# Two orders inside a planned recurrent step: which product comes first in its third tick, and where one relu stands among the evictions

## The chip, the cores and the metric

The kernel runs on one core of a Trainium2 chip. The metric is the device time of one execution in microseconds; lower is better. Engines are named as in the profile: PE is TensorE's matmul, PEld its weight load, DVE is VectorE, ACT is ScalarE, POOL is GpSimd, SP issues DMAs.

## What is computed

The input is 64 graphs of 256 nodes with 256 features (x) and an integer adjacency matrix each (adj). Two residual layers follow each other; the normalisation has no weights. Cut to what matters:

```python
# layer 0: a gated graph network, three steps with shared GRU weights
h = relu(layernorm(x))
for i in range(3):
    m    = h @ weight[i]
    aggr = einsum('bst,bsd->btd', adj != 0, m)
    gi, gh = aggr @ w_ih.T + b_ih, h @ w_hh.T + b_hh
    r = sigmoid(gi_r + gh_r)
    z = sigmoid(gi_z + gh_z)
    n = tanh(gi_n + r * gh_n)
    h = (1 - z) * n + z * h
x = x + h
# layer 1: graph attention, 4 heads of 64
v = (relu(layernorm(x)) @ W.T + b)
logits = leaky_relu(v.a_src[i] + v.a_dst[j], 0.2), masked where adj != 1
x = x + softmax(logits over j) @ v
```

## The kernel before, in words

**Work.** The graphs are taken in 32 pairs. A pair's state is held transposed, `hT`: 128 partitions (features, two chunks) by 512 columns (two graphs of 256 nodes). All products are fp32. Many of the GRU's products are not computed as they stand: the weights are combined beforehand (`w_a`, `w_h`, `w_n`) and sums of states are formed on DVE (`T1`, `T2`, `T3`, `T4`, and `T2n`, `T3n`, `T4n` for the n gate), so that the two graphs of a pair share some products. A call of `block` (L309) is such a product: four matmuls of 128x256, which the trace shows as eight records[...]. A call of `part` (L447) is one matmul (two records) of 128x256.

**The plan.** Every piece of work is a Python function put into `plan` at a tick, which may be a fraction, and a phase: STEP, READY, REST in that order (L322 to L328). At the end the ticks are run through in order (L1033), and the scheduler is manual (L123): what a function emits goes to the end of the queue of its engine. So each engine works in exactly the order in which the functions are called; waits between engines are put in by the framework. A step takes six ticks, `tick_0` to `tick_5` of the class `Step`. A pair has three steps, which start 12 ticks apart, and pairs start 18 ticks apart; so there is always exactly one step in hand, and between its ticks stand the other pairs' normalisation, transposes and attention. The pattern repeats every 18 ticks, that is every three steps. I call those three steps slot A, slot B and slot C, in the order of the trace.

**One step.** `tick_1` makes the part NS2 into one half of the bank `qb` (L482), has DVE write `qb`'s other half from it (L483), makes the block RH into `pc`, the part N01, and has ACT copy `pc` to `pd` (L489); DVE makes T3 and T2. `tick_2` (L494) makes the parts NS3 and NS4 into the two halves of `qb` (L496, L497), has DVE make a piece of `hn` from the first (L498, a scalar_tensor_tensor, "the stt" below) and ACT another from the second (L501, which runs as L451, "state_n"), then the block S1 from T1 into the bank `p5` (L502; the trace writes it `p<-T`), which ACT copies to `m5` (L503, in the trace `m<-p`), and DVE makes T4 (L504). `tick_3` makes the block S2 into `pd`, DVE adds `pd` and `m5` into the bank `pe` (L509, "the pe add"), then the block RA into `pc`. `tick_4` makes the part N11, the block RZ into `pd` (in the trace `pd<-T,w_h`; it overwrites what the pe add reads) and the block S4 into `pe` (it adds to what the pe add wrote). `tick_5` is the n gate and the tail; `update` (L552) makes the new state one step later.

**Beside the step.** When a step has ended, `back` (L788) turns each half of the new state back to nodes with four transposes (bank `pback`, L807), ACT rounds it to `hNhi` (L797) and DVE takes the rest, `hNlo` (L798). It stands in the REST phase of the ticks 1 and 2 of the step that follows; so the second half's `hNhi` and `hNlo` stand right behind `tick_2`. In slot C the last step of a pair has ended, and `residual` (L811) takes their place.

From the third pair on, the first normalisation is made ahead and turned by DMA: `result` makes `xn_a` (L353, four instructions on DVE), a relu in place on ACT follows (L771), and `halve` (L385) splits the result into half words (L387, `words_a`) for a DMA to DRAM and a transposing DMA back. `result` and the relu stand in the READY phase of tick -10 of their pair; that is `tick_2` of another pair's step, in slot B. `halve` stands in the READY phase of tick -9. In slot B stand also ACT's first masks of another pair's logits (L921, 128x1024) at that same tick 2, and the attention values: products `pv` (L863), DVE's `val` (L868) and `score` (L876), and a transpose of the scores on PE, `pscore` (L886).

In slot A stand ACT's leaky relus of the attention (L968) and DVE's row maxima (`any`, L948).

**PSUM.** Five banks rotate for the step (`ps_g`: qa, qb, pc, p5, pd, pe, pn0, pn1), three for all else (`ps_m`).

Of the kernel before, what the change touches and what calls it, by code (L numbers as in the profile page):

```python
# [14 lines left out]
AF = mybir.ActivationFunctionType  # L15
# [3 lines left out]
P = 128  # L19
# [8 lines left out]
def gated_gnn_then_gat_kernel(  # L28
# [39 lines left out]
    nc = tc.nc  # L68
    B, N, D = x.shape
# [4 lines left out]
    KD = D // P  # L74
# [3 lines left out]
    T = PB * N  # L78
# [121 lines left out]
    w_a = [const.tile([P, KD, 6 * D], F32, name=f"w_a_{l}") for l in range(L)]  # L200
    RH, RZ = range(2)
    N00, N01, N11, NS1, NS2, NS3, NS4 = range(7)
    RA, ZA, NA, S1, S2, S4 = range(6)
# [99 lines left out]
    def flat(y):  # L303
        return y.rearrange("q r d -> q (r d)")
# [4 lines left out]
    def block(pt, w, j, src, start=False):  # L309

        for c in range(KD):
            for k in range(KD):
                nc.tensor.matmul(  # L313
                    pt[:, ts(c, N)], w[:, k, j * D + c * P : j * D + (c + 1) * P], src[:, k, :],
                    start=start and c == 0 and k == 0, stop=(c == KD - 1 and k == KD - 1),
                    skip_group_check=True,
                )
# [9 lines left out]
    def at(tick, phase, p, fn):  # L327
        plan.setdefault(tick, ([], [], []))[phase].append((-p, fn))  # L328

    def plan_norm(src, name, p, ticks, relu=False):  # L330


        v = {}

        def stats(r0):
            def fn():
                if not v:
                    v["st"] = small.tile([P, R, 6], F32, tag="st", name=f"st_{name}")
                    v["mv"] = small.tile([P, R, 2], F32, tag="mv", name=f"mv_{name}")
                for r in (r0, r0 + 1):  # L340
                    nc.vector.bn_stats(v["st"][:, r, :], src()[:, r, :])
                    nc.vector.bn_aggr(v["mv"][:, r, :], v["st"][:, r, :])
            return fn

        def deviation():
            rstd = v["rstd"] = small.tile([P, R], F32, tag="rstd", name=f"rstd_{name}")
            nc.vector.tensor_scalar_add(rstd, v["mv"][:, :, 1], EPS)
            nc.gpsimd.tensor_tensor(rstd, rstd, mhalf, ALU.pow)

        def result():  # L350
            xn = v["xn"] = buf("xn", [P, R, D], f"xn_{name}")
            for r in range(R):
                nc.vector.tensor_scalar(  # L353
                    xn[:, r, :], src()[:, r, :], v["mv"][:, r, 0:1], 0.0 if relu else v["rstd"][:, r : r + 1],
                    op0=ALU.subtract, op1=ALU.max if relu else ALU.mult,
                )

        for t, fn in zip(ticks, (stats(0), stats(2), deviation, result)):
            at(t, READY, p, fn)
        return v  # L360

    def plan_relu_T(v, tag, name, p, ticks):

        w = {}

        def fn(k):
            def go():
                if not w:
                    w["hT"] = buf(tag, [P, KD, T], f"hT_{name}")
                pt = bank(f"pt_{name}_{k}")  # L370
                for r in range(R):
                    nc.tensor.transpose(pt[:, ts(r, P)], v["xn"][:, r, ts(k, P)], ident)
                nc.scalar.activation(w["hT"][:, k, :], pt, AF.Relu)
            return go

        for k, t in enumerate(ticks):
            at(t, REST, p, fn(k))
        return w

    def plan_turn(src, tag, name, p, ticks):  # L380


        w = {}

        def halve():  # L385
            words = buf("words", [P, R, 2, D], f"words_{name}", U16)
            nc.vector.tensor_copy(words, src().bitcast(U16).rearrange("q r (d w) -> q r w d", w=2))  # L387
            w["rows"] = dram.tile([R, P, 2 * D], U16, tag="words", name=f"words_dram_{name}")
            nc.sync.dma_start(w["rows"].rearrange("r q e -> q r e"), words.rearrange("q r w d -> q r (w d)"))

        def turn():
            w["turned"] = buf("turned", [P, 2, KD * T], f"turned_{name}", U16)
            nc.sync.dma_start_transpose(
                w["turned"].rearrange("q w (k n) -> q (w k) n", k=KD), w["rows"].rearrange("r q e -> (r q) e")
            )

        def join():
            w["hT"] = buf(tag, [P, KD, T], f"hT_{name}")
            nc.vector.tensor_copy(
                flat(w["hT"]).bitcast(U16).rearrange("q (n w) -> q n w", w=2), w["turned"].rearrange("q w n -> q n w")  # L400
            )

        at(ticks[0], READY, p, halve)
        at(ticks[1], REST, p, turn)
        at(ticks[2], READY, p, join)
        return w
# [4 lines left out]
    def of(y, i):  # L411
        return y[:, :, ts(i, N)]

    class Step:
# [77 lines left out]
            nc.vector.tensor_add(self.own("T2", [P, KD, N]), T3, h0)  # L492

        def tick_2(self):  # L494
            q_b = self.qb
            self.part(q_b[:, :N], NS3, self.T3n)  # L496
            self.part(q_b[:, N:], NS4, of(self.hT(), 1)[:, 1, :])  # L497
            nc.vector.scalar_tensor_tensor(  # L498
                of(self.hn, 1)[:, 1, :], q_b[:, :N], bhn[:, 1:2], self.m5n, op0=ALU.add, op1=ALU.add
            )  # L500
            self.state_n(0, 1, q_b[:, N:])  # L501
            block(self.p5, w_a[self.l], S1, self.T1, start=True)  # L502
            nc.scalar.copy(self.own("m5", [P, T]), self.p5)  # L503
            nc.vector.tensor_sub(self.own("T4", [P, KD, N]), self.T2, of(self.aggr, 0))  # L504

        def tick_3(self):
            R_ = self.own("R", [P, KD, T])
# [232 lines left out]
    def plan_pair(p):  # L740
# [5 lines left out]
        def ready(t, fn):  # L746
            at(t0 + t, READY, p, fn)
# [20 lines left out]
        xn_a = plan_norm(lambda: v["x"], f"a{p}", p, [t0 + t for t in norm_ticks])  # L768
        ready(-1 if p else -2.5, to_edge)
        if dma_a:  # L770
            ready(-10, lambda: nc.scalar.activation(flat(xn_a["xn"]), flat(xn_a["xn"]), AF.Relu))  # L771
            h = plan_turn(lambda: xn_a["xn"], "hT_a", f"a{p}", p, [t0 - 9, t0 - 8, t0 - 3])
        else:
            h = plan_relu_T(xn_a, "hT_a", f"a{p}", p, [t0 - 4, t0 - 3])
# [238 lines left out]
    for p in range(NPAIR):  # L1013
        plan_pair(p)
# [52 lines left out]
```

## Time and profile before

| what | value |
|---|---|
| median of 3 runs | 2521.81 us (2521.77 to 2523.39) |
| the profiled execution | 2522.01 us, span 2520.2 us |
| PE / PEld busy | 2468.9 us (98%) / 2189.5 us (87%) |
| DVE / ACT / POOL busy | 1947.3 us (77%) / 1433.9 us (57%) / 630.3 us (25%) |
| granted TensorE clock | 0.997 |
| a block (eight records), start to start | 1.73 us |
| a part (two records), start to start | 0.43 us |
| a period of three slots | 76.4 us |
| the profile's chain by engine | PE 68%, DVE 23%, ACT 6% |

The period is the distance of two neighbouring `pscore` matmuls in the timeline, 1254.19 and 1330.64 us. A line of a timeline reads: start in the span, duration, engine, line of the kernel, operation, the tile written, the tiles read, shapes, how many instructions are merged, and in brackets the idle time before it and what ended that. In a list of waits, a line reads: who waited for whom, the time in all, how often, the longest.

### The profile page before, as it was taken

The page shows a single profiled execution, that of the slowest core. Times are in us where ns is not written, and L with a number is a line of the kernel's source. Part 1 is how long each engine was busy: PE and PEld are TensorE (multiplying, and loading weights), DVE is VectorE, ACT ScalarE, POOL GpSimd, SP SyncE. Part 2 cuts the span into 40 slices and gives each one's busy share as a digit, 9 for nine tenths or more (in the row PEclk, how much of TensorE's full clock was granted, in tenths as well). Part 3 has the DMA queues.
Part 4 walks back from the last instruction along what each step waited for, and adds up shares of the span by engine and source line. Part 5 has one row for each costly group of instructions (what it writes and reads, how often), then busy time and mean ns, then how long its engine had stood idle before and what let it go on. Part 6 is the DMA issues. An engine that isn't in the chain of part 4 may idle for free.

```text
span 2520.2 us, 37693 instructions
## 1 busy us (share of the span) xinstructions
PE 2468.9 (98%) x13446; PEld 2189.5 (87%) x13446; DVE 1947.3 (77%) x4576; ACT 1433.9 (57%) x3007; POOL 630.3 (25%) x514
## 2 busy tenths in 40 slices
PE   8999999999999999999999999999999999999998
PEld 6888888888888888888888888888888888888887
DVE  5678877788777788777878777887777887778767
ACT  3445556555555555556555555555565555665664
POOL 0112232222222232222232322222222222222222
PEclk9999999999999999999999999999999999999999
DMA  3025656555656455656556565556565556564455
GB/s 95 17 59 126 152 117 143 128 124 127 155 114 150 119 124 137 135 125 145 116 128 149 122 139 131 121 126 159 109 151 120 126 133 135 126 148 118 107 115 109
DMA packets 322091, 313.73 MB, mean 124 GB/s; under 512 B 166560, under 2 KB 282224, under 8 KB 321904
## 3 DMA queue, kind: packets, MB, share of 16 engines
q1 hardware_dynamic: 286608, 181.29, 27.1%
q0 software_dynamic: 33728, 130.03, 26.9%
q8 instruction: 106, 1.74, 0.3%
q14 instruction: 81, 0.66, 0.1%
q10 hardware_dynamic: 1568, 0.01, 0.0%
HBM read 215.62 MB, written 56.60 MB: 108 GB/s over the span
## 4 chain that ended last, share of the span: by engine, by line
PE 68%; DVE 23%; ACT 6%; issue 2%; DMA 1%; POOL 0%; DVEq 0%; SPq 0%; ACTq 0%; POOLq 0%
PE pd L313 16%; PE pn L313 9%; PE pc L313 9%; PE po L572 7%; PE pe L313 6%; PE qb L448 5%; PE pa L470 5%; PE p L313 4%; PE qa L448 3%; DVE any L948 3%; DVE hT_a L558 2%; DVE val L868 2%; DVE edge L763 2%; DVE hNlo L798 2%; PE pback L807 2%
## 5 line engine op out<-in xcount | busy, mean ns | idle before, releaser
L540 POOL TENSOR_TENSOR R<-hT_a,hn 128x512 f32<-128x512 f32 x191 | 278.2, 1457 | 1250.2 <-ACT hn L536 1175.5
L313 PE MATMUL pn<-aggr,w_a 128*128 128x256 f32 x1536 | 365.1, 380 | 1.8 <-DVE pn L525 1.8
L313 PE MATMUL pd<-T,w_a 128*128 128x256 f32 x1536 | 366.3, 381 | 0.0
L313 PEld LDWEIGHTS pn<-aggr,w_a 128*128 128x128 f32 x1536 | 286.9, 190 | 43.2 <-DVE pn L525 3.2
L313 PEld LDWEIGHTS pd<-T,w_a 128*128 128x128 f32 x1536 | 288.1, 191 | 37.6
L557 DVE SCALAR_TENSOR_TENSOR R<-Z,R 128x512 f32<-128x512 f32 x192 | 134.3, 700 | 215.9 <-POOL R L540 207.5
L572 PEld LDWEIGHTS po<-val,zz 128*128 128x128 f32 x2048 | 244.9, 192 | 4.5
L948 DVE CUSTOM_DVE_ANT_0 any<-drow,noedge 128x256 f32<-128x256 f32 x496 | 238.0, 480 | 9.7 <-DMA drow<-score_dram 1.0
L536 ACT ACTIVATE hn<-pn,bi 128x256 f32<-128x256 f32 x384 | 160.3, 470 | 146.0 <-PE pn L313 145.8
L572 PE MATMUL po<-val,zz 128*128 128x65 f32 x2048 | 242.1, 272 | 0.0
L588 POOL TENSOR_TENSOR x<-x,o 128x256 f32<-128x256 f32 x124 | 136.9, 1105 | 393.3 <-DVE o L583 372.1
L968 ACT ACTIVATE zz<-zz,val 128x256 f32<-128x256 f32 x496 | 224.2, 506 | 0.0
L455 ACT ACTIVATE R<-pc,brz 128x256 f32<-128x256 f32 x192 | 80.5, 470 | 241.6 <-PE pc L313 241.6
L798 DVE TENSOR_TENSOR hNlo<-pback,hNhi 128x512 fp32r<-128x512 f32 x128 | 88.2, 689 | 150.4 <-ACT hNhi L797 150.4
L455 ACT ACTIVATE R<-pe,brz 128x256 f32<-128x256 f32 x192 | 80.5, 470 | 216.2 <-PE pe L313 216.2
L525 DVE SCALAR_TENSOR_TENSOR pn<-R,hn 128x512 f32<-128x512 f32 x192 | 148.6, 774 | 49.3 <-ACT R L455 32.0
L313 PE MATMUL pd<-T,w_h 128*128 128x256 f32 x768 | 183.6, 382 | 0.2 <-DVE pe L509 0.2
L313 PE MATMUL p<-T,w_a 128*128 128x256 f32 x768 | 181.4, 379 | 0.0
L313 PE MATMUL pc<-hT_a,w_h 128*128 128x256 f32 x768 | 181.4, 379 | 0.0
L313 PE MATMUL pc<-aggr,w_a 128*128 128x256 f32 x768 | 181.4, 379 | 0.0
L313 PE MATMUL pe<-aggr,w_a 128*128 128x256 f32 x768 | 181.4, 379 | 0.0
L313 PEld LDWEIGHTS pd<-T,w_h 128*128 128x128 f32 x768 | 143.5, 190 | 24.7 <-DVE pe L509 6.4
(183 smaller groups left out, 5254.8 us busy)
## 6 DMA issues: line engine op xcount, KB each, us to landing
zz<-score_dram POOLq DMA_DIRECT2D x62, 1024.0 KB, 11.8
zz<-topT_dram POOLq DMA_DIRECT2D x62, 1024.0 KB, 8.8
adj<-in_adj_dram SPq DMA_DIRECT2D x64, 512.0 KB
drow<-score_dram SPq DMA_DIRECT2D x62, 512.0 KB
x<-in_x_dram SPq DMA_DIRECT2D x32, 512.0 KB
out_dram<-x SPq DMA_DIRECT2D x31, 512.0 KB
words_dram_a<-words_a SPq DMA_DIRECT2D x30, 512.0 KB
words_dram_b<-words_b SPq DMA_DIRECT2D x29, 512.0 KB
```

What stands on the lines that cost most here:

```text
L313: nc.tensor.matmul(pt[:, ts(c, N)], w[:, k, j * D + c * P : j * D + (c + 1) * P], src[:, k, :], start=start and c == 0 and k == 0, stop=(c ...
L448: nc.tensor.matmul(pt, w_n[:, j, :], src, start=start, stop=True, skip_group_check=True)
L455: nc.scalar.activation(of(dst, i)[:, c, :], src[:, c, :], AF.Tanh, bias=brz[:, g0 + c : g0 + c + 1], scale=0.5)
L525: nc.vector.scalar_tensor_tensor(by_c(self.bank(f"pn{i}")), of(self.R, i), 1.0, of(self.hn, i), op0=ALU.add, op1=ALU.mult)
L536: nc.scalar.activation(n__[:, c, :], p_n[:, c, :], AF.Tanh, bias=bi[:, 2 * KD + c : 2 * KD + c + 1])
L540: nc.gpsimd.tensor_sub(of(self.R, i), of(self.hT(), i), n__)
L557: nc.vector.scalar_tensor_tensor(d_, of(self.Z, i), 1.0, d_, op0=ALU.add, op1=ALU.mult)
L572: nc.tensor.matmul(po[:, ts(h_, VC)], zz[:, j, h_, ts(s, P)], v["val"][:, i * KN + j, ts(h_, VC)], start=(j == 0), stop=(j == KN - 1),)
L588: add(v["x"][:, r, :], v["x"][:, r, :], o)
L798: nc.vector.tensor_sub(lo, pt, hi)
L948: nc.vector.tensor_tensor_reduce(any_, drow[r // KN][:, h, :], v["noedge"][:, r, :], 1.0, -3.0e38, ALU.add, ALU.max, accum_out=v["top"][:, ...
L968: nc.scalar.activation(zz[:, h, :], zz[:, h, :], AF.Prelu, alpha=ALPHA, bias=v["val"][:, r, S0 + H + h : S0 + H + h + 1],)
```

## The change

Two edits. In `tick_2` the block S1 and ACT's copy of it to `m5` are called ahead of the parts NS3 and NS4, and T4 is made ahead of the stt; so on PE the order is S1, NS3, NS4, on ACT `m5`, state_n, and on DVE T4, the stt. This holds for all 96 steps. And the relu of `xn_a` goes from tick -10 to tick -9.5, which puts it behind everything of tick -10: on ACT, behind the masks (L921) and behind the second `hNhi` of slot B. This holds for the 30 pairs that are turned by DMA. The numbers of instructions stay the same on every engine, and the orders on POOL and on SP stay as they were.

```diff
         def tick_2(self):
+
             q_b = self.qb
+            block(self.p5, w_a[self.l], S1, self.T1, start=True)
+            nc.scalar.copy(self.own("m5", [P, T]), self.p5)
             self.part(q_b[:, :N], NS3, self.T3n)
             self.part(q_b[:, N:], NS4, of(self.hT(), 1)[:, 1, :])
+            nc.vector.tensor_sub(self.own("T4", [P, KD, N]), self.T2, of(self.aggr, 0))
             nc.vector.scalar_tensor_tensor(
                 of(self.hn, 1)[:, 1, :], q_b[:, :N], bhn[:, 1:2], self.m5n, op0=ALU.add, op1=ALU.add
             )
             self.state_n(0, 1, q_b[:, N:])
-            block(self.p5, w_a[self.l], S1, self.T1, start=True)
-            nc.scalar.copy(self.own("m5", [P, T]), self.p5)
-            nc.vector.tensor_sub(self.own("T4", [P, KD, N]), self.T2, of(self.aggr, 0))
...
         if dma_a:
-            ready(-10, lambda: nc.scalar.activation(flat(xn_a["xn"]), flat(xn_a["xn"]), AF.Relu))
+            ready(-9.5, lambda: nc.scalar.activation(flat(xn_a["xn"]), flat(xn_a["xn"]), AF.Relu))
             h = plan_turn(lambda: xn_a["xn"], "hT_a", f"a{p}", p, [t0 - 9, t0 - 8, t0 - 3])
```

## The prediction

> **What bounds the kernel now.** I read the busy shares first, then the waits, then PE's timeline over one period, and last DVE, ACT and the weight loads in the same window.
>
> ```profile
> PE 2468.9 (98%) x13446; PEld 2189.5 (87%) x13446; DVE 1947.3 (77%) x4576; ACT 1433.9 (57%) x3007; POOL 630.3 (25%) x514
> ```
>
> PE is the bound: what can be gained by a new order is PE's idle time, some tens of microseconds. The list of waits says where the recurring part lies:
>
> ```profile
> ACT hn L451 <- DVE hn L498: 123.4, 66, 2.2
> PEld qb L448 <- DVE qb L483: 23.5, 28, 1.0
> PE qb L448 <- DVE qb L483: 16.8, 28, 0.7
> PE pscore L886 <- DVE score L876: 7.1, 29, 0.8
> PEld pd L313 <- DVE pe L509: 6.4, 29, 0.6
> ```
>
> 28 times, so once in a period, the part NS3 waits for DVE's write of qb (slot A); 29 times pscore waits for the score (slot B). Slot C has none. PE's timeline prices slot A:
>
> ```profile
> 1220.94 0.60 PE L807 MATMUL pback<-ident,hT_a 128*128 128x128 f32 x4
> 1222.14 0.70 PE L448 MATMUL qb<-T3n,w_n 128*128 128x256 f32 x2 [0.60 <-DVE qb L483]
> 1223.11 1.89 PE L313 MATMUL p<-T,w_a 128*128 128x256 f32 x8
> ```
>
> In slot C the transposes start at 1268.88 and NS3 at 1269.32, 0.44 later, and S1 at 1270.18, 0.86 after NS3. Undisturbed, S1 would start in slot A at 1220.94 + 0.44 + 0.86 = 1222.24; it starts at 1223.11. The wait costs 0.87 us, 28 times: 24.4 us.
>
> What stands next in slot A, on DVE, on ACT and at the weight loads:
>
> ```profile
> 1224.74 0.47 DVE L498 SCALAR_TENSOR_TENSOR hn<-qb,bhn,m5n 128x256 f32<-128x256 f32 x1
> 1225.13 0.68 DVE L504 TENSOR_TENSOR T<-T,aggr 128x512 f32<-128x512 f32 x1
> 1227.50 0.69 DVE L798 TENSOR_TENSOR hNlo<-pback,hNhi 128x512 fp32r<-128x512 f32 x1 [0.55 <-ACT hNhi L797]
> 1228.11 0.69 DVE L509 TENSOR_TENSOR pe<-pd,m 128x512 f32<-128x512 f32 x1
> ```
>
> ```profile
> 1225.24 0.47 ACT L451 ACTIVATE hn<-qb,bhn 128x256 f32<-128x256 f32 x1 [1.79 <-DVE hn L498]
> 1225.62 0.57 ACT L503 COPY m<-p 128x512 f32<-128x512 f32 x1
> 1226.08 0.91 ACT L968 ACTIVATE zz<-zz,val 128x256 f32<-128x256 f32 x2
> 1226.89 0.58 ACT L797 CAST hNhi<-pback 128x512 fp32r<-128x512 f32 x1
> ```
>
> ```profile
> 1228.95 1.70 PEld L313 LDWEIGHTS pd<-T,w_h 128*128 128x128 f32 x8
> ```
>
> The reader is to see a second chain: the stt ends at 1225.21, state_n starts at 1225.24, then m5, two leaky relus, hNhi; hNlo waits for that, and the pe add stands behind it and ends at 1228.80. The block RZ loads its weights at 1228.95. Where that load does wait for the pe add (slot B, below), it starts 0.06 after its end; so the slack is 0.15 - 0.06 = 0.09 us. The distance is 0.14 or 0.15 in all 28 periods.
>
> Slot B, with the relu in front of the masks and hNhi:
>
> ```profile
> 1249.83 1.06 ACT L771 ACTIVATE xn_a<-xn_a 128x1024 f32<-128x1024 f32 x1 [0.94 <-DVE xn_a L353]
> 1250.79 1.04 ACT L921 ACTIVATE zz<-link 128x1024 f32<-128x1024 bf16 x1
> 1251.74 0.56 ACT L797 CAST hNhi<-pback 128x512 fp32r<-128x512 f32 x1
> ```
>
> ```profile
> 1254.19 0.27 PE L886 MATMUL pscore<-ident,score 128*32 128x128 f32 x1 [0.22 <-DVE score L876]
> ```
>
> hNlo (1252.34), two vals and the score follow hNhi; the score ends at 1254.04. The block RA before pscore starts at 1252.08, so pscore was due at 1252.08 + 1.73 = 1253.81. Then RZ's load waits for the pe add, which stands behind the score (1253.95 to 1254.64): it starts at 1254.70, and S4 starts at 1256.53, 1.83 later. Undisturbed: 1253.81 + 0.11 (pscore) + 0.43 (N11) + 1.73 (RZ) = 1256.08. Slot B loses 0.45 us.
>
> **What the Trainium skill says.** "PSUM — Partial Sum Buffer", section on PSUM bank collisions: accesses of two engines to one bank and quadrant have to be kept apart by semaphores, two reads too. The trace agrees: state_n reads the other half of qb than the stt, and yet starts 0.03 us after the stt's end. "TensorE: Matmul & The Clock Gate", the architectural detail on the array: DVE and ACT are strict FIFOs, PE pulls only weight loads ahead. The trace agrees: the pe add starts only when hNlo ahead of it has had its hNhi, though pd was complete about 1 us before (its block started at 1225.28 and shows 1.89). "SBUF — State Buffer", section on who interferes with whom: a GpSimd instruction can block DVE for its whole length. The trace agrees: in slot A one `any` takes 1.49 us beside POOL's work, the next 0.42.
>
> **The change part by part.** Times are of this one profiled execution, in the slots above.
>
> *S1 ahead of the parts, slot A.* S1 reads T1, which DVE made at 1213.34, and needs nothing of DVE's queue here. It starts at 1220.94 + 0.44 = 1221.38, runs 1.73, NS3 starts at 1223.10, NS4 at 1223.53; DVE's write of qb ended at 1222.09, so that wait is gone and PE is 0.87 ahead. Next late is the pe add. DVE is in backlog: hNlo's first half at 1224.13 and what stands before are unchanged. Then T4 starts at 1224.74 and takes 0.60 start to start, the stt starts at 1225.34 and ends at 1225.81 (NS4 ends at 1223.53 + 0.59 = 1224.12, no wait). State_n starts at 1225.84. m5 is out of the way (S1's last matmul ends about 1223.26), so the leaky relus start 0.38 later at 1226.22, hNhi 0.81 later at 1227.03, and ends at 1227.60. hNlo 1227.64, pe add 1228.25 to 1228.94. That is 0.14 later than before: T4 in front costs 0.60, m5 out of the way gives 0.46. RZ's weights, now wanted at 1228.95 - 0.87 = 1228.08, load at 1229.00; S4 starts at 1230.83, and before it started at 1230.89. **Of 0.87 us, 0.06 is left**: 28 x 0.06 = 1.7 us. N11 ahead of it needs T4n (about 1226.15) and state_n (1226.31) by 1227.6: no wait.
>
> *The relu, slot B.* PE: S1 1245.52, NS3 1247.25, NS4 1247.68 with its end at 1248.27. DVE: T4 at 1247.43; the stt waits for NS4 (one bank), 1248.32 to 1248.79; xn_a from 1248.71 to about 1250.0, 0.29 later than before. ACT: state_n 1248.82, the masks 1249.20 instead of 1250.79, hNhi 1250.15 to 1250.71. DVE: hNlo 1250.75, vals 1251.36, score at 1252.28 to 1252.45; pscore is due at 1253.81. The pe add ends about 1253.05, RZ is due at 1254.35. Both waits go: 28 x 0.45 = 12.6 us. One early slot has the relu but no score; there RZ's load waited 0.57 at 121.38 and S4 gains 0.43. Cover of the relu itself: it runs from about 1250.6 to 1251.7, while ACT's next (R, 1254.01) waits for PE; halve stands behind the pe add at 1253.0 and doesn't wait. Without that cover it would cost its 1.06. Halve's DMA keeps its place on SP's queue and starts about 1.5 us earlier; no queue on SP or POOL is passed.
>
> *Slot C.* S1 starts at 1269.32, NS4 ends at 1271.48 + 0.59 = 1272.07; the stt starts at 1272.12 instead of 1270.38, and T4n and all behind it on DVE 1.13 later. Before the pe add DVE idles 1.21 (waiting for PE's pd), which takes it up; and after it RZ leaves 2.76. State_n waits for that stt, and behind it is queued only an exp (L983, 1272.59, now about 1273.0), wanted by a product at 1283.26. Cost: nothing; without DVE's idle time 1.13 a period would still lie inside the 2.76.
>
> *Sum.* 1.7 + 12.6 + 0.4 = 14.7 us, from 2522.01 to 2507.3 in the profiled execution; the median is 0.2 lower, so **2507.1 us**. Not shown by the trace is ACT's and DVE's exact start in slot A after the reordering: I give 0.1 us a period either way, 2.8 us, and 1 us for the first and last pairs: 2503 to 2511.
>
> **The rivals.**
> - *Slot A's wait really goes.* If hNhi's second half did not hang on the stt, the whole 0.87 would come: 28 x 0.81 = 22.7 more, 2484. For it: the qb wait is the largest on PE. Against it: ACT's queue, with state_n 0.03 after the stt, and RZ's 0.09 of slack. Chance 0.10.
> - *Slot B gives nothing back.* The stt behind NS4 holds up xn_a, state_n and the masks, so that the score is late again: 2507.1 + 12.6 = 2519.7. Against it: the score would have to be 1.3 us later than I have it. Chance 0.08.
> - *Slower.* In slot A the pe add slips further, because a DVE instruction between 1224.74 and 1228.9 falls beside POOL work and takes 1.49 for 0.42, as one does at 1215.22: 28 x 1.07 = 30, 2537. It decides from 14.7 / 28 = 0.52 us a period on. For it: the chain has no slack. Against it: POOL idles from 1218.99 to 1236.04. Chance 0.05.
> - That the order doesn't change as the diff says is excluded: the built program has it on PE, DVE and ACT.
>
> **How the numbers follow.** My forecast has 0.77. The range 2498 to 2514 takes in its own 2503 to 2511 and a part of the neighbours, and leaves out about 0.2. 0.2% is 5.0 us, about what a measurement of this kernel can tell from no change. Faster by more: 0.77 + 0.10 and a little of the second rival, 0.88; within: 0.07; slower: 0.05.
>
> **What would show it.** In the profile after, the wait of PE's qb for L483 is gone, and in its place PE and PEld wait about 28 times for the pe add, with about 0.8 to 0.9 us each on the weight load; pscore's 28 waits are gone; the period is 0.5 us shorter. Wrong would be: no new wait at RZ (then 2484), pscore still waiting, or RZ's wait over 1.4.

## The result, and the profile after

The changed kernel takes **2509.53 us** (median; 2508.47 to 2515.74), the kernel before on the same chip 2521.81 us (2521.42 to 2528.7). The ratio is 0.9949 [0.9935, 0.9963]: 12.3 us faster, where 14.7 were predicted (2507.1 us). The profiled execution took 2509.14 us, its span is 2507.3 us; before, 2522.01 and 2520.2 us. A few executions of several kernels here, the one before among them, take some 7 us longer, with a granted clock of 0.994 or 0.995 instead of 0.996 to 0.999, which matters below only where two medians of one kernel differ.

The busy line of the page after hardly shows it (PE's share of the span stays at 98%):

```profile
PE 2463.9 (98%) x13446; PEld 2191.4 (87%) x13446; DVE 1956.2 (78%) x4576; ACT 1437.7 (57%) x3007; POOL 629.8 (25%) x514
```

The list of waits does. The lines of qb for L483 and of pscore for the score are gone, and there is more waiting for the pe add. (The changed kernel has one line more, so what was L509 is L510 here, and so on.)

```profile
ACT hn L451 <- DVE hn L502: 107.6, 96, 2.0
...
PEld pd L313 <- DVE pe L510: 26.4, 29, 1.3
...
PE pd L313 <- DVE pe L510: 14.9, 28, 0.9
```

Before, RZ's load waited 6.4 us for the pe add; now 26.4, and 28 of the 29 cases are slot A's. PE's timeline there:

```profile
1216.74 0.60 PE L808 MATMUL pback<-ident,hT_a 128*128 128x128 f32 x4
1217.17 1.89 PE L313 MATMUL p<-T,w_a 128*128 128x256 f32 x8
1218.90 0.59 PE L448 MATMUL qb<-T3n,w_n 128*128 128x256 f32 x2
...
1224.76 1.99 PE L313 MATMUL pd<-T,w_h 128*128 128x256 f32 x8 [0.50 <-DVE pe L510]
```

From the transposes to NS3 there is no gap. But RZ's weights load 1224.76 - 1216.74 = 8.02 us after the transposes, and before it was 1228.95 - 1220.94 = 8.01. The time won ahead of S1 is lost again ahead of RZ; only S4 follows a little sooner, 1.83 us after that load instead of 1.94. DVE and ACT in the same window:

```profile
1220.53 0.68 DVE L501 TENSOR_TENSOR T<-T,aggr 128x512 f32<-128x512 f32 x1
1221.12 0.47 DVE L502 SCALAR_TENSOR_TENSOR hn<-qb,bhn,m5n 128x256 f32<-128x256 f32 x1
...
1223.40 0.69 DVE L799 TENSOR_TENSOR hNlo<-pback,hNhi 128x512 fp32r<-128x512 f32 x1 [0.54 <-ACT hNhi L798]
1224.01 0.69 DVE L510 TENSOR_TENSOR pe<-pd,m 128x512 f32<-128x512 f32 x1
```

```profile
1219.15 0.59 ACT L498 COPY m<-p 128x512 f32<-128x512 f32 x1
1221.63 0.47 ACT L451 ACTIVATE hn<-qb,bhn 128x256 f32<-128x256 f32 x1 [1.90 <-DVE hn L502]
1222.00 0.90 ACT L969 ACTIVATE zz<-zz,val 128x256 f32<-128x256 f32 x2
1222.80 0.57 ACT L798 CAST hNhi<-pback 128x512 fp32r<-128x512 f32 x1
```

The chain is the predicted one, link by link: the stt ends at 1221.59, state_n starts 0.04 later, then the leaky relus, hNhi, hNlo, the pe add (ends 1224.70), and RZ's load starts 0.06 after that.

In slot B the order on ACT is now state_n, masks, hNhi, relu, and pscore (PE's timeline, second fence) has no wait:

```profile
1244.89 1.05 ACT L922 ACTIVATE zz<-link 128x1024 f32<-128x1024 bf16 x1
1245.84 0.57 ACT L798 CAST hNhi<-pback 128x512 fp32r<-128x512 f32 x1
1246.30 1.07 ACT L772 ACTIVATE xn_a<-xn_a 128x1024 f32<-128x1024 f32 x1
```

```profile
1249.50 0.27 PE L887 MATMUL pscore<-ident,score 128*32 128x128 f32 x1
```

Where the 12.9 us between the two spans lie was worked out slot by slot, from the start of a step's first `qa<-T` to the start of its S4, after against before. Slot A is 0.08 to 0.10 shorter in nearly every period, slot B 0.45 to 0.47 in all, slot C 0.00 to 0.01. When the ninth step (a slot A, the first of the steady part) reaches S4, the changed kernel is **2.5 us behind**, and 12.0 us ahead at the last step. So the steady part gains 14.5 us (27 x 0.085 + 28 x 0.46 = 15.2, less 0.35 for each of two single slots A, near 758 and 1745 us, that are 0.26 and 0.27 longer than before), and 2.5 us are lost in the first eight steps. The two single slots come with the moved relu: the kernel with the relu alone has both, at 0.36 and 0.35 us more than before, the one with the order alone has neither. Why, the runs don't tell. The last 0.9 us of the 12.9 come behind the last S4; I did not take them apart.

### The profile page after: what moved, and what is told of

The parts are those of the page before. It is cut to its first block, busy times and chain, and to the rows that moved or that the text cites. A ratio compares the mean times of both kernels' runs of the same rounds, so it can differ in the third digit from the quotient of the medians.

```text
span 2507.3 us, 37756 instructions
## 1 busy us (share of the span) xinstructions
PE 2463.9 (98%) x13446; PEld 2191.4 (87%) x13446; DVE 1956.2 (78%) x4576; ACT 1437.7 (57%) x3007; POOL 629.8 (25%) x514
## 4 chain that ended last, share of the span: by engine, by line
PE 74%; DVE 21%; ACT 2%; issue 1%; DMA 0%; POOL 0%; DVEq 0%; SPq 0%; POOLq 0%
PE pd L313 16%; PE pn L313 9%; PE pc L313 9%; PE po L573 7%; PE pe L313 6%; PE pa L470 5%; PE qb L448 5%; PE p L313 5%; PE pv L864 5%; PE qa L448 4%; DVE any L949 4%; PE pback L808 2%; DVE hT_a L559 2%; DVE edge L764 2%; DVE R L558 2%; DVE hNlo L799 1%
## 5 line engine op out<-in xcount | busy, mean ns | idle before, releaser
L313 PEld LDWEIGHTS pd<-T,w_h 128*128 128x128 f32 x768 | 143.5, 190 | 44.7 <-DVE pe L510 26.4
L313 PEld LDWEIGHTS pc<-aggr,w_a 128*128 128x128 f32 x768 | 145.9, 190 | 19.9
```

What stands on the lines that cost most here:

```text
L313: nc.tensor.matmul(pt[:, ts(c, N)], w[:, k, j * D + c * P : j * D + (c + 1) * P], src[:, k, :], start=start and c == 0 and k == 0, stop=(c ...
```

## The experiments

Theory: in slot A two waits stand in series on PE; the edit in `tick_2` takes the first, and the second, the chain stt, state_n, hNhi, hNlo, pe add, gives back nearly all of it. The relu brings nearly all of the gain. Rivals: the gain is slot A's after all; or RZ's wait has another cause than that chain.

### The relu alone

On the kernel before:

```diff
-            ready(-10, lambda: nc.scalar.activation(flat(xn_a["xn"]), flat(xn_a["xn"]), AF.Relu))
+            ready(-9.5, lambda: nc.scalar.activation(flat(xn_a["xn"]), flat(xn_a["xn"]), AF.Relu))
```

> The relu at tick -9.5, tick_2 as before the change. Theory (the two edits act apart: the relu gives slot B its 0.45 us, the tick_2 edit gives slot A under 0.1 us a period and costs about 2 us in the first slots): 28 x 0.45 + 0.4 = 13.0 less than before, 2508.8 us; pscore's waits gone, the 28 waits of PE for DVE's write of qb all still there. Rival (the gain needs both edits, or comes from the tick_2 edit): 2518 to 2522.

Measured: 2508.68 us (2508.32 to 2511.27), ratio 0.9944 [0.993, 0.9957]. Slot B is 0.46 shorter, slot A unchanged but for the two single ones, and the first steps lose nothing (0.03 us). Its list of waits still has slot A's:

```profile
PEld qb L448 <- DVE qb L483: 24.2, 28, 1.2
...
PE qb L448 <- DVE qb L483: 17.5, 28, 1.0
```

One moved instruction brings as much as the whole change.

### The order in tick_2 alone

On the changed kernel:

```diff
-            ready(-9.5, lambda: nc.scalar.activation(flat(xn_a["xn"]), flat(xn_a["xn"]), AF.Relu))
+            ready(-10, lambda: nc.scalar.activation(flat(xn_a["xn"]), flat(xn_a["xn"]), AF.Relu))
```

> The tick_2 edit, the relu at tick -10 as before the change. Theory: slot A gains 0.08 a period (2.2 us); in slot B the stt waits for NS4, so xn_a and the relu end 0.3 us later and pscore with them, 28 x 0.29 = 8 us more; the first slots cost 2.3: about 2530 us, slower than before. Rival (the tick_2 edit carries the gain): 2509 to 2515.

Measured: 2531.79 us (2531.3 to 2533.28), ratio 1.0034 [1.0021, 1.0046]: alone, this edit makes the kernel **slower**. Slot A is 0.06 to 0.09 shorter, slot B 0.29 longer, because there the stt now waits for NS4 and on ACT state_n, the relu, the masks and hNhi come later, and so does the score. The first eight steps lose 4.5 us; 1.0 of that is in two early slots B, which the moved relu spares the changed kernel. So the two edits don't add up: with the relu moved, slot B has the slack that this one uses.

### Slot A's chain, a link at a time

Four kernels, each on the changed one. First T4 behind the stt, as it was before; S1 and m5 stay in front:

```diff
-            nc.vector.tensor_sub(self.own("T4", [P, KD, N]), self.T2, of(self.aggr, 0))
             nc.vector.scalar_tensor_tensor(
                 of(self.hn, 1)[:, 1, :], q_b[:, :N], bhn[:, 1:2], self.m5n, op0=ALU.add, op1=ALU.add
             )
             self.state_n(0, 1, q_b[:, N:])
+            nc.vector.tensor_sub(self.own("T4", [P, KD, N]), self.T2, of(self.aggr, 0))
```

> As after the change, but T4 stands behind the stt again. Theory (slot A's gain is eaten through stt, state_n, hNhi, hNlo, pe add; T4 in front is 0.60 us of it): the pe add ends 0.60 earlier, S4 in slot A starts about 0.5 to 0.6 us earlier per period: 28 x 0.5 to 0.6 less, 2493 to 2496 us; the weight load's wait for the pe add falls from 0.92 to about 0.3 us. Rival (the pe add is late because of DVE's backlog as a whole, in whatever order the two stand): within 2 us of after, 2507.5 to 2511.5.

Measured: 2493.81 us (2492.95 to 2494.7), ratio 0.9883 [0.9869, 0.9896]. Slot A is 0.58 to 0.60 shorter than in the changed kernel; T4 takes 0.59 from start to start there (1220.53 to 1221.12). RZ's wait shrinks by as much:

```profile
PEld pd L313 <- DVE pe L510: 10.2, 29, 0.7
```

Then the other way: m5 behind state_n, as it was before, T4 stays in front:

```diff
             block(self.p5, w_a[self.l], S1, self.T1, start=True)
-            nc.scalar.copy(self.own("m5", [P, T]), self.p5)
             self.part(q_b[:, :N], NS3, self.T3n)
...
             self.state_n(0, 1, q_b[:, N:])
+            nc.scalar.copy(self.own("m5", [P, T]), self.p5)
```

> As after the change, but on ACT state_n stands ahead of the m5 copy again. Theory (m5 out of the way is worth 0.46 us on the chain to the pe add): hNhi's second half in slot A 0.46 later, S4 0.48 later per period: 28 x 0.48 = 13 us more than after, 2523 us; the weight load's wait in slot A about 1.4 us. Rival (ACT has room there): 2509.5 us.

Measured: 2523.95 us (2522.93 to 2530.98), ratio 1.001 [1.0001, 1.0018]: the whole gain of the change is gone. Slot A is 0.49 to 0.50 longer than in the changed kernel, and the wait grows by as much:

```profile
PEld pd L313 <- DVE pe L510: 40.4, 30, 1.8
```

Beside that 2.2 us are lost in the third step and 1.7 come back ahead of the last. The clock accounts for most of both: from 95 to 105 us the granted clock is 0.66 here and 0.83 in the changed kernel, by estimate 10 x 0.17 = 1.7 us; ahead of the last step it is 1.00 here (2430 to 2470 us) and 0.96 there (2415 to 2455), 40 x 0.04 = 1.6 us. The two runs show that RZ waits for this chain: what is put in front of the stt on DVE, or behind state_n on ACT, appears in that wait to within 0.03 us (T4 0.59 in the timeline and 0.58 in the wait, m5 0.47 and 0.50).

Third, the link itself. State_n reads the other half of a bank than the stt, and still starts only when the stt has ended; ACT's queue stands behind it. Its result is wanted only in `tick_5`, and N11 is the first product that writes the bank again, so it can be issued a tick later, behind hNhi:

```diff
-            self.state_n(0, 1, q_b[:, N:])
 
         def tick_3(self):
             R_ = self.own("R", [P, KD, T])
+            self.state_n(0, 1, self.qb[:, N:])
             block(self.pd, w_a[self.l], S2, self.T2)
```

> As after the change, but state_n of tick_2 is called at the start of tick_3, behind slot A's second hNhi; T4 stays in front of the stt. Theory (the chain to the pe add runs over state_n): hNhi no longer hangs on the stt, the pe add follows DVE's row maxima at once and ends about 1228.2 on the old scale; RZ's load waits about 0.2 instead of 0.92 us, S4 0.72 earlier per period: 28 x 0.72 = 20 less than after, 2489 us. Rival (DVE's backlog alone sets the pe add): 2509 us.

Measured: 2497.79 us (2490.66 to 2498.0), ratio 0.9898 [0.9884, 0.9911]; the profiled execution took 2490.66 us, the three others 7 us more. So I ran it again:

> The same kernel as the one with state_n late, a second time: its profiled execution took 2490.7 us, three others 2497.7 to 2498.0. If the shorter is the kernel's own time, most of these runs take 2490 to 2491 us. If the theory is missing something that costs 7 us in this order of the work, most take about 2498, and a profile of one of them would show where, for instance as a wait of 0.25 us in each period.

Measured: 2490.12 us (2489.78 to 2496.89), ratio 0.9872 [0.9855, 0.9888]. This time the profiled execution was a longer one, with a span of 2495.1 us, and RZ's wait was the same (8.6 us, 28 times; 9.2, 29 times in the shorter). The last S4 starts at 2432.25 us in it and at 2432.30 in the shorter, so all of the difference lies behind that; there the granted clock is 0.50 from 2443 to 2460 us, and 1.00 in the shorter. So the 7 us are the clock's, not the order's, and 2490 is the time to compare. Slot A is 0.61 shorter than in the changed kernel (0.63 in the second profile); I had expected 0.72.

Fourth, that and T4 behind the pe add:

```diff
-            nc.vector.tensor_sub(self.own("T4", [P, KD, N]), self.T2, of(self.aggr, 0))
...
             nc.vector.tensor_add(self.bank("pe"), self.pd, self.m5)
+            nc.vector.tensor_sub(self.own("T4", [P, KD, N]), self.T2, of(self.aggr, 0))
             block(self.pc, w_a[self.l], RA, of(self.aggr, 0))
```

> As the kernel with state_n late, and T4 besides goes to tick_3, behind the pe add. Theory: the pe add is 0.60 earlier still, no wait at RZ is left in slot A, the whole 0.87 us of the qb wait comes in (0.79 more than after, 28 times 22.1), and DVE has room again in the early slot C that lost 1.0 us: about 2486.4 us. Rival (another wait takes its place, for instance N11 for state_n or T4n): 2489 or more, with that wait in the list about 28 times.

Measured: **2485.74 us** (2485.68 to 2485.81), ratio 0.9857 [0.9843, 0.987], the fastest of all. Slot A is 0.78 shorter than in the changed kernel, so 0.86 to 0.87 than before: the whole price of the first wait. That is 28 x 0.78 = 21.8 of the 23.8 us between the two medians; in the profiled executions another 1.7 us lie ahead of the last step, where the clock again is 1.00 (2395 to 2430 us) instead of 0.96. They are not the order's: the kernel with state_n late has them in its first profile and not in its second. Its lists of waits, of ACT and of PE:

```profile
ACT hn L451 <- DVE hn L501: 6.9, 30, 0.8
```

```profile
PE pn L313 <- DVE pn L526: 3.5, 3, 1.9
```

ACT waits 6.9 us for the stt, 107.6 in the changed kernel and 20.5 with state_n late alone; RZ's wait is gone but for three single ones, and PE's largest wait is three early ones. One expectation failed: the loss in an early slot C (below) did not come back but grew by 0.54. There the stt waits for NS4 with nothing in front of it, since T4, which had filled that wait, now stands behind (the stt waits 1.66 us there instead of 1.07, and the product `pn` behind it 1.93 instead of 1.33); T4 in front costs where DVE is in backlog and helps where it waits. The 0.54 itself isn't all of that: the granted clock is 0.50 from 219 to 221 us in this execution, in the same slot.

### Without the first edit

If the chain is all, S1 need not stand in front. The fastest kernel, with S1 and m5 put back behind the parts:

```diff
             q_b = self.qb
-            block(self.p5, w_a[self.l], S1, self.T1, start=True)
-            nc.scalar.copy(self.own("m5", [P, T]), self.p5)
             self.part(q_b[:, :N], NS3, self.T3n)
...
+            block(self.p5, w_a[self.l], S1, self.T1, start=True)
+            nc.scalar.copy(self.own("m5", [P, T]), self.p5)
```

> As the kernel with state_n and T4 late and the relu moved, but S1 and its copy stand behind the parts as before the change. Theory (two waits in series: the qb wait on PE and the pe add; taking one away brings nothing as long as the other stands): the 28 qb waits are back at 0.60 us, slot A is as long as before, 28 x 0.45 + 0.4 from slot B alone: 2508.5 us. Rival (the order of the products doesn't matter once the chain to the pe add is short): 2487 us.

Measured: 2513.2 us (2510.76 to 2513.34), ratio 0.9963 [0.995, 0.9977]. The first wait is back, and dearer than before (23.5 us there):

```profile
PEld qb L448 <- DVE qb L483: 27.2, 28, 1.3
```

So all that was gained at the chain is lost at qb: neither wait brings as much as 0.1 us a period alone, both together 0.87. It is also 4.7 us over what I expected. Slot A is 0.12 longer than before, 28 x 0.12 = 3.4 us: in slot C, T4 behind the pe add uses up the 0.41 us for which DVE waited for po before, and its backlog into slot A starts that much later. Of the other 1.3 us the profile shows 0.60 behind the eighth step, where with T4 late the product `pn` waits 0.90 us for DVE instead of 0.21 before, 0.21 in the first step and 0.15 behind the fifth; the rest I did not find.

### The first step

In the changed kernel S1 of the very first step reaches PE before its weights are made (PE's timeline):

```profile
30.39 0.59 PE L313 MATMUL p<-T,w_a 128*128 128x256 f32 x2
31.59 1.56 PE L313 MATMUL p<-T,w_a 128*128 128x256 f32 x6 [0.60 <-DVE w_a L247]
```

The first step in the old product order, all others as changed:

```diff
+            if self.n_ != "0_0":
                 block(self.p5, w_a[self.l], S1, self.T1, start=True)
                 nc.scalar.copy(self.own("m5", [P, T]), self.p5)
             self.part(q_b[:, :N], NS3, self.T3n)
             self.part(q_b[:, N:], NS4, of(self.hT(), 1)[:, 1, :])
+            if self.n_ == "0_0":
+                block(self.p5, w_a[self.l], S1, self.T1, start=True)
+                nc.scalar.copy(self.own("m5", [P, T]), self.p5)
```

> As after the change, but in the first step alone S1 stands behind the parts. Theory (S1 in front waits in the first slot for the weights that DVE is still combining, 0.86 us): PE's wait for w_a in the first S1 goes, and the second step starts 0.9 us earlier than after, 57.2 instead of 58.1 us of the span. Rival (the first slot's loss is the DMA's scatter): no change beyond it.

Measured once: 2507.34 us. The wait for w_a is gone. From the group of products ahead of it to S2 it is 33.29 - 25.54 = 7.75 us, in the changed kernel 33.85 - 25.23 = 8.62: 0.87 us. The second step starts only 0.55 us earlier, since this execution was 0.3 late before that group already. The total says little about it: of the two profiled executions this one is 2509.14 - 2507.34 = 1.8 us shorter, but 1.7 us are won ahead of the last step, where the clock is 1.00 (2400 to 2450 us) instead of 0.96.

## Why the prediction was right, and where it was off

**Slot A, right.** "Of 0.87 us, 0.06 is left": 0.085 measured. The two terms of it, T4 +0.60 and m5 -0.46, are shown one by one: 0.59 and 0.49. With the transposes' starts put on each other (4.20 us apart), the pe add ends at 1228.90 of the old trace; 1228.94 was foretold. RZ's load waits 0.91 or 0.92 us in nearly every period; 0.8 to 0.9 was named. The chain is shown by four kernels, and the rival that slot A's wait really goes is out. It takes another change: state_n and T4 moved as well (2485.74, near that rival's 2484; about 1.7 us of it is the clock's, see above).

The Trainium skill counts two reads of one bank and quadrant among the accesses that semaphores have to keep apart ("PSUM — Partial Sum Buffer", section on bank collisions), which fits state_n's hanging on the stt. The stt itself behaves alike: in slot C it starts 0.04 us after NS4's end (207.81 + 0.59 = 208.40, and 208.44), though NS4 writes only the half of the bank that the stt doesn't read. But state_n and the stt also write one tile, `hn`, in different parts, and no run here has the one without the other; that the bank is the reason is argued, not shown. The runs show the consequence: 107.6 us of ACT's waiting, and what stands behind it in a strict order, worth 28 x 0.61 = 17 us on PE.

**Slot B, right.** 0.45 predicted, 0.46 measured, and 0.43 in the one early slot, as predicted. The rival in which it gives nothing back is what happens to the order of `tick_2` without the relu: +0.29 a period.

**Slot C, right in 28 periods, wrong in one early slot.** The stt is late there as foretold, and S4 comes to 0.00. But the eighth step of all is a slot C in which no attention of an earlier pair runs yet, and DVE has no idle time there: the working took a period from the middle for every slot. Its reserve, that the delay would lie inside RZ's 2.76 us even without DVE's idle time, looked at RZ alone; what is late is the product `pn` two products behind it, which waits for DVE too. DVE's timeline, then PE's, in the changed kernel:

```profile
208.44 0.48 DVE L502 SCALAR_TENSOR_TENSOR hn<-qb,bhn,m5n 128x256 f32<-128x256 f32 x1 [1.07 <-PE qb L448]
...
211.17 0.69 DVE L814 TENSOR_TENSOR x<-pback,x 128x512 f32<-128x512 f32 x1
211.77 0.69 DVE L510 TENSOR_TENSOR pe<-pd,m 128x512 f32<-128x512 f32 x1
...
216.73 0.69 DVE L526 SCALAR_TENSOR_TENSOR pn<-R,hn 128x512 f32<-128x512 f32 x1
```

```profile
214.35 1.89 PE L313 MATMUL pe<-aggr,w_a 128*128 128x256 f32 x8
217.57 1.97 PE L313 MATMUL pn<-aggr,w_a 128*128 128x256 f32 x8 [1.33 <-DVE pn L526]
```

and PE's in the kernel before:

```profile
214.87 2.00 PE L313 MATMUL pn<-aggr,w_a 128*128 128x256 f32 x8 [0.21 <-DVE pn L525]
```

The stt waits 1.07 us for NS4, the pe add follows its predecessor without a gap, everything behind on DVE is 1 us later, and the product `pn` waits 1.33 instead of 0.21 us. The slot costs 1.03 us.

**The first pairs, mis-sized.** "1 us for the first and last pairs" stood for all of this, either way. Measured, the first eight steps lose 2.5 us net: 1.44 in the first step (0.87 of it the wait for w_a; 0.58 lies between its `qa<-T` and the product `pmT`, 2.48 us instead of 1.90, which both stand ahead of `tick_2`, so that the edit can't reach them), 0.38 in the third (a product that waits for hNlo 1.28 instead of 0.89 us, at the end of the same chain from the stt), 1.03 behind the eighth, and 0.25 of scatter ahead of them all, less 0.43 gained in the relu's early slot and 0.18 in another. So the order itself costs about 2.1 us there (0.87 + 0.38 + 1.03 - 0.18), and 0.8 are scatter. The relu alone has none of these losses, the order of `tick_2` alone has all. That is the miss: 14.7 predicted, 12.3 measured on medians; the steady part's 14.5 us stand against 14.3 of the sum (1.7 + 12.6).

**The slower rival** didn't come: no DVE instruction in slot A's chain got longer; POOL was idle there as read.

## What to carry to other kernels

Where an engine is the bound, before taking its largest wait away, follow the same stretch to the next instruction that has to wait for another engine, and write down its slack: here 0.87 us shrank to 0.085 because the next load had 0.09 to spare, and only both together brought 0.87. Look for an instruction that holds a strict queue for a reason of its own (here a shared bank or a shared tile) while nobody wants its result yet: issued a tick later, it brought more than the reorder. And work an order that holds for all steps through the first steps as well; they have neither the idle time nor the ready weights of the middle.

## What I had not expected of the hardware

- DVE's next instruction after the stt starts 0.39 us after it when it is T4 (1224.74 and 1225.13 before), and 0.51 when it is T4n (1221.12 and 1221.63 after; also 1210.58 and 1211.08, 0.50, in the fastest kernel). So T4 starts 0.08 before the stt's end and T4n 0.03 or 0.04 after it. The kernel has a reason for it, which no run tests: T4n is put into the buffer of `m5n` (L442; there is one such buffer), and the stt reads `m5n`. It is small, but slot A counts hundredths.
- The granted clock is halved for short stretches, not at the same places in every execution: it is 0.50 from 219 to 221 us in the fastest kernel's profile, and 0.50 from 2443 to 2460 in the longer profile of the one with state_n late. In the changed kernel's it is 0.76 from 2429 to 2436, by estimate 7 x 0.24 = 1.7 us, against 28 x 0.085 = 2.4 us that slot A gains in the whole run. So a small difference between two profiled executions is looked for in the clock first, stretch by stretch.
